# Attention and mixture of experts on one core: value products in two parts, maxima and statistics one at a time

## The chip, the cores and the metric

The kernel runs on one NeuronCore of a Trainium2 chip. The core has a matrix engine (TensorE, PE in the profile; its weight loads are shown as PEld), a vector engine (VectorE, DVE), a scalar engine (ScalarE, ACT), GpSimd (POOL) and an engine that mostly issues DMAs (SyncE, SP). [...] The metric is the device time of one execution in microseconds; the median of three runs is given.

## The reference

The input x has 2 sequences of 1024 positions and 256 channels, in float32. One layer is computed: causal attention with 16 query heads of 16 channels, 4 key and value heads and a linear position bias; a residual and a layer norm; then a mixture of 8 experts with the best one per token beside a shared expert; a residual and a second layer norm. Cut to what matters:

```python
q, k, v = x @ Wq, x @ Wk, x @ Wv              # 16 heads, 4 kv heads, 16 channels each
att = einsum("bhqd,bhkd->bhqk", q, k) / sqrt(16) + alibi + causal
att = softmax(att, axis=-1)
x = layernorm(x + einsum("bhqk,bhkd->bhqd", att, v) @ Wo)
logits = x @ router_w.T                       # the best expert, weighted by its sigmoid
routed = (up * silu(gate)) @ down             # of that expert
shared = (silu(x @ shared_gate) * (x @ shared_up)) @ shared_down
out = layernorm(x + shared + routed)
```

## The kernel before

The attention works on query tiles of 128 positions, 8 for each of the two sequences: `(b, qt)`. The softmax needs the maximum of each row before anything is exponentiated, so the scores are computed twice. Once as `s_ps` (queries on partitions, `start_s` and `end_s`, L403 to L469), only for the row maxima. Once as `t_ps` (keys on partitions, `start_t` and `end_t`, L497 to L539), with the maximum already subtracted by way of one more channel of the query (`qS`, L491), for the exponentials. One key tile of one query tile, `(b, qt, kt)`, is a step; there are 72 steps, the diagonal one first in each query tile.

The order of all instructions is written out by hand in Python. A counter `slot` goes up by one in every gap. For each step with scores still to be made there are two bursts, one per pair of kv heads, and after each a gap (L891 to L904). A burst is two `t_ps` matmuls for this step and two `s_ps` units for a query tile some steps ahead, interleaved. All four write PSUM banks of one pool of six (`ps_st`, tag `st`), taken in turn. ACT empties the `t_ps` banks: it exponentiates them into `pT` (L521), or, on the diagonal, copies them to `pD` (L524), which POOL masks (L526) before ACT exponentiates it (L538). DVE empties the `s_ps` banks with maximum reductions into `past` (L436). Where a unit holds a diagonal block, DVE (L449) and ACT (L451) also copy that block to `diag`; once it is complete, POOL masks one half of it, and DVE takes its four maxima (L466), one for each kv head, in slots that L464 and L465 fix by number.

`gap` (L813) puts other work between two bursts, in this order: what is due by its slot (`after_burst`, L770); at most one product that is due (`product`, L541); `join_maxima` and `spread_maxima` (L473, L483), which bring the row maxima into the query of a coming tile by way of the transposes `mT`; and one of the pieces of `finish` (L563), if there is room. A product multiplies the exponentials of one step with the values. It is four matmuls, one for each kv head, each 32 output partitions by 512 columns, into the accumulator `yT`, which is one PSUM bank of its own. When a query tile's last product is done, `finish` goes through its pieces in later gaps: a copy of `yT` to `y_raw`, four transposes `yq`, the division by the row sums (`y_n`), the transposes `ytp`, the output projection `o_ps`, the residual and the layer norm (`layernorm`, L223), the transposes `x1tp`, and the router's `lg`. With `room` at 0, no piece with PE work is placed; the old `gap` sets that after `mT`, and after a product when there is little to finish.

Ten bursts of `s_ps` alone come first, among the projections. When no scores are left to make, ten wide gaps (L825) hold the rest of the steps, each with one piece of the shared expert (`shared_pieces`, L695: `gu_sh`, `h_sh`, `dp_sh`), and last gaps (L842) the remainder. After `route` (L631) and the scatters of rows, the expert part (from L926) runs over the experts one by one, with the weights coming in by DMA.

## Time and profile before

| | |
|---|---|
| time, median of 3 runs | 580.52 us (579.5 to 581.03) |
| the profiled execution | 580.1 us, of which the span from the first to the last instruction is 578.3 us |
| mean granted TensorE clock | 0.99 |
| busy over the span | PE 552.6 us (96%), DVE 346.8 us (60%), ACT 266.8 us (46%), POOL 161.0 us (28%) |
| 0 to 56 us | projections and the ten leading bursts: PE 52.7 us busy, DVE 32.8, ACT 18.2 |
| 56 to 326 us | bursts and gaps |
| 326 to 428 us | wide gaps and the end of the attention: PE 101.0 us busy, DVE 45.7, ACT 42.8 |
| 428 to 578.3 us | experts: PE 131.8 us busy, DVE 59.9, POOL 73.1 |
| chain that ended last | PE 86%, DVE 6%, ACT 3% of the span |

The costliest groups of instructions are the two kinds of scores and what empties them. In this view a row has the line, engine, operation, what is written and read, the shape, the count, then the time in which at least one of them ran, the mean length of one in ns, and the idle time of the engine before them with what ended most of it.

```profile
L417 PE MATMUL s_ps<-kT,qT 32*128 32x512 f32 (+2 forms) x896 | 184.5, 470 | 1.8 <-ACT diag L451 0.8
L436 DVE TENSOR_REDUCE past<-s_ps 128x1 f32<-128x512 f32 (+3 forms) x256 | 148.0, 617 | 57.5 <-PE s_ps L417 50.1
L502 PE MATMUL t_ps<-qS,kT 32*128 32x512 f32 x576 | 168.4, 637 | 0.3 <-ACT pD L524 0.3
L521 ACT ACTIVATE pT<-t_ps 128x512 f32<-128x512 f32 x224 | 121.4, 600 | 76.3 <-PE s_ps L417 50.1
```

A float32 matmul of the program stands in the trace as two records: the 288 `t_ps` matmuls of the program are the 576 of L502. Matmuls that use different rows or columns of the array run at the same time, so the lengths of their records add up to more than the time they take; what counts is the distance from the start of one group to the start of the next.

### The profile page before, as it was taken

What the parts mean: (1) busy time and instruction counts of PE and PEld (TensorE: products, weight loads), DVE (VectorE), ACT (ScalarE), POOL (GpSimd) and SP (SyncE); (2) the same over time, 40 slices, a digit from 0 to 9 for tenths busy, and PEclk for the clock granted to TensorE, in tenths of its full rate; (3) what the DMA queues carried; (4) which work ended last, traced back from release to release, by engine and by line L of the source; (5) the groups of instructions that cost most, each with busy time, mean ns of one, the idle gap of its engine ahead of it and who ended that gap; (6) DMA issues with size and microseconds to landing.
All of it is one profiled execution on the core that took longest, in us unless ns stands there. A gap on an engine that the chain in (4) does not pass through costs nothing.

```text
span 578.3 us, 8805 instructions
## 1 busy us (share of the span) xinstructions
PE 552.6 (96%) x3292; PEld 305.5 (53%) x3292; DVE 346.8 (60%) x829; ACT 266.8 (46%) x509; POOL 161.0 (28%) x192
## 2 busy tenths in 40 slices
PE   8999999999999999999999999999999899999990
PEld 4655443534334353435345535446566788888650
DVE  2398968687696867688768733334542354544540
ACT  3432877657666756656667656461111111111120
POOL 5310511210201110114312301411020357776541
PEclk9999999999999999999999999999999999999996
DMA  6222850000000000000100000101071845552100
GB/s 201 42 34 36 233 180 2 2 1 0 2 1 1 1 1 1 2 2 31 44 1 1 1 1 19 56 0 38 8 278 57 285 150 173 183 194 71 46 17 3
DMA packets 24638, 34.72 MB, mean 60 GB/s; under 512 B 3806, under 2 KB 19460, under 8 KB 24592
## 3 DMA queue, kind: packets, MB, share of 16 engines
q1 hardware_dynamic: 20320, 27.38, 15.7%
q0 software_dynamic: 3456, 6.34, 3.1%
q8 instruction: 28, 0.46, 0.3%
q10 hardware_dynamic: 816, 0.39, 0.2%
q14 instruction: 18, 0.15, 0.1%
HBM read 22.20 MB, written 12.97 MB: 61 GB/s over the span
## 4 chain that ended last, share of the span: by engine, by line
PE 86%; DVE 6%; ACT 3%; issue 1%; DMA 1%; POOL 0%; POOLq 0%; ACTq 0%; DVEq 0%
PE t_ps L502 19%; PE yT L546 11%; PE s_ps L417 10%; PE gu_sh L705 6%; PE gp L1137 5%; PE dp L1153 5%; PE up L1137 5%; PE dp_sh L725 4%; PE o_ps L591 3%; DVE past L436 3%; PE qpj L291 3%; PE kpj L291 1%; PE mT L487 1%; PE dp L1195 1%; PE gp L1045 1%; PE lg L616 1%
## 5 line engine op out<-in xcount | busy, mean ns | idle before, releaser
L417 PE MATMUL s_ps<-kT,qT 32*128 32x512 f32 (+2 forms) x896 | 184.5, 470 | 1.8 <-ACT diag L451 0.8
L436 DVE TENSOR_REDUCE past<-s_ps 128x1 f32<-128x512 f32 (+3 forms) x256 | 148.0, 617 | 57.5 <-PE s_ps L417 50.1
L502 PE MATMUL t_ps<-qS,kT 32*128 32x512 f32 x576 | 168.4, 637 | 0.3 <-ACT pD L524 0.3
L521 ACT ACTIVATE pT<-t_ps 128x512 f32<-128x512 f32 x224 | 121.4, 600 | 76.3 <-PE s_ps L417 50.1
L417 PEld LDWEIGHTS s_ps<-kT,qT 32*128 32x128 f32 x896 | 79.3, 184 | 16.8 <-DVE past L436 4.9
L502 PEld LDWEIGHTS t_ps<-qS,kT 32*128 32x128 f32 x576 | 52.0, 183 | 59.4 <-issue 31.0
L231 POOL TENSOR_TENSOR rstd<-rstd,neg_half 128x1 f32<-128x1 f32 x36 | 20.5, 570 | 151.2 <-DVE rstd L230 149.7
L546 PE MATMUL yT<-pT,v 128*32 128x512 f32 x448 | 59.7, 605 | 0.0
L526 POOL TENSOR_SCALAR_AFFINE_SELECT pD<-pD 128x1024 f32<-128x1024 f32 x32 | 34.8, 1096 | 77.6 <-ACT pD L524 77.5
L524 ACT COPY pD<-t_ps 128x512 f32<-128x512 f32 x64 | 34.4, 600 | 20.0 <-PE s_ps L417 14.6
L705 PE MATMUL gu_sh<-x1T,sh_gu 128*128 128x512 f32 x96 | 43.6, 597 | 0.0
L237 POOL DMA_INDIRECT slot_x<-xs,slots x32 | 32.1, 1002 | 41.2 <-DVE slots L686 28.1
L454 POOL TENSOR_SCALAR_AFFINE_SELECT diag<-diag 128x1024 f32<-128x1024 f32 x16 | 17.5, 1097 | 92.9 <-ACT diag L451 92.9
L466 DVE TENSOR_REDUCE past<-diag 128x4 f32<-128x512 f32 x64 | 41.9, 676 | 0.0
L1145 ACT ACTIVATE sg<-gp 128x512 f32<-128x512 f32 x16 | 9.6, 597 | 54.6 <-PE gp L1137 44.3
L538 ACT ACTIVATE pD<-pD 128x1024 f32<-128x1024 f32 x32 | 34.3, 1072 | 0.4 <-POOL pD L526 0.4
L451 ACT COPY diag<-s_ps 128x128 f32<-128x128 f32 (+2 forms) x64 | 23.9, 377 | 22.5 <-DVE past L436 19.9
L1137 PE MATMUL gp<-slot_xT,wgu 128*128 128x256 f32 x128 | 30.4, 381 | 1.2 <-ACT slot_xT L1106 1.2
L449 DVE TENSOR_TENSOR diag<-s_ps,causal 128x128 f32<-128x128 f32 (+2 forms) x64 | 26.4, 415 | 7.1 <-PE s_ps L417 7.0
L1137 PE MATMUL up<-slot_xT,wgu 128*128 128x256 f32 x128 | 30.2, 379 | 0.0
L1153 PE MATMUL dp<-wd,slot_h 128*128 128x256 f32 x128 | 29.0, 379 | 0.0
L1082 POOL DMA_INDIRECT zt<-z_dram,row x20 | 20.6, 1032 | 27.8 <-issue 27.5
(171 smaller groups left out, 657.4 us busy)
## 6 DMA issues: line engine op xcount, KB each, us to landing
wgu<-_L_ffn_gate_up_proj_dram SPq DMA_DIRECT2D x8, 1024.0 KB
wd<-in_L_ffn_down_proj_dram SPq DMA_DIRECT2D x8, 512.0 KB
slot_x<-empty SPq DMA_DIRECT2D x1, 3900.0 KB
row<-slot_x SPq DMA_DIRECT2D x8, 260.0 KB
xs<-in_L_attn_x_dram SPq DMA_DIRECT2D x4, 512.0 KB
qT<-q_all SPq DMA_DIRECT2D x32, 64.0 KB
z_dram<-z_sh SPq DMA_DIRECT2D x12, 128.0 KB
row<-slot_x SPq DMA_DIRECT2D x4, 130.0 KB
```

The costliest lines, as they stand in the source:

```text
L417: lambda r=r: nc.tensor.matmul(sp[:, r * n * P : (r + 1) * n * P], lhsT=qT[b][rows, r0 + r, ts(qt, P)], rhs=kT[b][rows, key * P : (key + n ...
L436: nc.vector.tensor_reduce(past[:, h * HALF + j, heads, parts[b, qt][key]], sp[j][:, :, : past_n * P], AX.X, ALU.max, negate=True,)
L466: lambda g=g: nc.vector.tensor_reduce(past[:, g, :, 0], diag[:, g], AX.X, ALU.max, negate=True),
L502: lambda: nc.tensor.matmul(tp, lhsT=kT[b][rows, ts(kt, P)], rhs=qS[b, qt][rows].rearrange("p r q -> p (r q)"), start=True, stop=True,)
L521: nc.scalar.activation(p[:, j], tp[j], AF.Exp)
L524: nc.scalar.copy(p[:, j], tp[j])
L526: nc.gpsimd.affine_select(out=p, in_=p, pattern=[[0, HALF * REP], [1, P]], compare_op=ALU.is_ge, fill=MASKED, base=0, channel_multiplier=-1,)
L538: lambda: nc.scalar.activation(p, p, AF.Exp),
L546: nc.tensor.matmul(yTs[b, qt][g * PAD : (g + 1) * PAD], lhsT=vs[b][:, kt, g, :], rhs=p[:, g, :], start=start, stop=stop,)
L705: nc.tensor.matmul(gu[k], lhsT=sh_gu[:, c, col : col + P], rhs=x1T[:, c, ts(tb, TB)], start=(c == 0), stop=(c == KC - 1),)
L1137: nc.tensor.matmul(dst[:, j], lhsT=wgu[:, e, c, col : col + P], rhs=xT[:, c, :], start=(c == 0), stop=(c == KC - 1),)
L1153: nc.tensor.matmul(dp, lhsT=h[:, f, ts(i, P)], rhs=wd[:, e, f, :], start=(f == 0), stop=(f == FC - 1),)
```

## The change

A product becomes two, each over 256 of the 512 columns (`k` is 0 or 1), queued one slot apart. `gap` places one that is due, then maxima or a piece, and, if no piece with PE work was placed, a second one that has been due for a slot. The first half of a new query tile waits until two slots after the end of the tile before (`y_free`), since `yT` is one bank. In a wide gap up to two are placed together. A piece may now also stand in a gap with a product; the old rule that sets `room` to 0 after a product is gone.

The maxima of diagonal blocks (L466 before) go into a list, `chores`. At the end of each gap `chore` runs one of them, unless the slot is in `with_chore`: the slots in which DVE has a `qS` addition, a `y_n`, the residual after `o_ps`, or the statistics of a layer norm. What is left of them for a query tile runs at once when its maxima are joined, when a later tile needs the buffer of an older one, or before the first `gu_sh` piece. The statistics of the layer norm (`bn`, `mv`, `rstd`) move from the gap of `o_ps` to the next slot, and the normalization to two slots after that.

```diff
@@ -403,6 +403,9 @@
         def start_s(unit, h, j):
             b, qt, r0, nr, key, n = unit
             if (b, qt) not in rowmax:
+                for c in [c for c in chores if c[1] != next(reversed(rowmax))]:
+                    chores.remove(c)
+                    c[2]()
                 rowmax[b, qt] = (
                     mp.tile([P, N_KV, REP, P], F32, tag="diag", name="diag"),
                     mp.tile([P, N_KV, REP, 4], F32, tag="past", name="past", bufs=6),
@@ -461,17 +464,23 @@
                 channel_multiplier=1,
             )
             for g in range(N_KV):
-                at(
-                    slot + (1 + g // 2 if slot < 0 or (b and qt < 2) else 2 + g),
-                    lambda g=g: nc.vector.tensor_reduce(
-                        past[:, g, :, 0], diag[:, g], AX.X, ALU.max, negate=True
-                    ),
+                chores.append(
+                    (
+                        slot + (1 if slot < 0 else 2),
+                        (b, qt),
+                        lambda g=g: nc.vector.tensor_reduce(
+                            past[:, g, :, 0], diag[:, g], AX.X, ALU.max, negate=True
+                        ),
+                    )
                 )
 
         qS = {}
 
         def join_maxima(b, qt):
 
+            for c in [c for c in chores if c[1] == (b, qt)]:
+                chores.remove(c)
+                c[2]()
             past = rowmax.pop((b, qt))[1]
             nc.vector.tensor_reduce(
                 mnegs[qt % 2][:, :, :, ROW_MAX].rearrange("p r g -> p g r"),
@@ -490,6 +499,7 @@
             q = mp.tile([P, REP, P], F32, tag="qS", name="qS")
             nc.vector.tensor_add(q, qT[b][:, :, ts(qt, P)], mT)
             qS[b, qt] = q
+            with_chore.add(slot)
 
 
         probs, yTs = {}, {}
@@ -538,19 +548,23 @@
                 lambda: nc.scalar.activation(p, p, AF.Exp),
             )
 
-        def product(b, qt, kt, start, stop):
-            p = probs.pop((b, qt, kt))
-            if start:
+        def product(b, qt, kt, k, start, stop):
+            nonlocal y_free
+
+            p = probs[b, qt, kt] if k == 0 else probs.pop((b, qt, kt))
+            if start and k == 0:
                 yTs[b, qt] = ps_y.tile([P, 512], F32, tag="y", name="yT")
             for g in range(N_KV):
                 nc.tensor.matmul(
-                    yTs[b, qt][g * PAD : (g + 1) * PAD],
+                    yTs[b, qt][g * PAD : (g + 1) * PAD, ts(k, 256)],
                     lhsT=vs[b][:, kt, g, :],
-                    rhs=p[:, g, :],
-                    start=start,
-                    stop=stop,
-                )
-            if stop:
+                    rhs=p[:, g, ts(k, 256)],
+
+                    start=start and k == 0,
+                    stop=stop and k == 1,
+                )
+            if stop and k == 1:
+                y_free = slot + 2
                 posts.append([slot + 1, finish(b, qt)])
                 posts[-1].append(next(posts[-1][1]))
 
@@ -571,6 +585,7 @@
             yq = small_tile([P, REP, N_KV, PAD], "yq")
             for r in range(REP):
                 nc.tensor.transpose(yq[:, r].rearrange("p g d -> p (g d)"), y_raw[:, r, :], ident)
+            with_chore.add(slot)
             rs = stat.tile([P, REP, N_KV], F32, tag="rs", name="rs")
             nc.vector.reciprocal(rs, yq[:, :, :, HD])
             nc.vector.tensor_mul(
@@ -592,20 +607,24 @@
                     o_ps, lhsT=y_nT[:, c, :], rhs=wo_sb[:, c, :], start=(c == 0), stop=(c == KC - 1)
                 )
             nc.vector.tensor_add(xs[:, tt, :C], xs[:, tt, :C], o_ps)
-            norm = [layernorm(xs[:, tt, :C])]
-
-            def end_norm():
+            with_chore.add(slot)
+            norm = [lambda: norm.append(layernorm(xs[:, tt, :C]))]
+
+            def go_on():
                 if norm:
                     norm.pop()()
 
             if s_queue:
-                at(slot + 2, end_norm)
+                with_chore.add(slot + 1)
+                at(slot + 1, go_on)
+                at(slot + 3, go_on)
                 yield 1, 4
             else:
-                end_norm()
+                go_on()
+                go_on()
 
                 yield 1, 1 + slot % 2
-            end_norm()
+            go_on()
             tp = small_tile([P, KC, P], "x1tp")
             for c in range(KC):
                 nc.tensor.transpose(tp[:, c, :], xs[:, tt, ts(c, P)], ident)
@@ -697,6 +716,9 @@
 
             def gate_and_up(f):
                 if not h:
+
+                    while chores:
+                        chores.pop(0)[2]()
                     h.append(mp.tile([P, FC, TB], F32, tag="diag", name="h_sh"))
                 gu = [bank("gu_sh") for k in range(2)]
                 for k in range(2):
@@ -750,6 +772,9 @@
         s_queue = [u for b, qt in order for u in s_units(b, qt)]
         slot = 0
         deferred, posts, products = [], [], []
+
+        chores, with_chore = [], set()
+        y_free = 0
         seen, routed = set(), 0
         bursts_left = True
         tail = [p for tb in (0, 1, 3) for p in shared_pieces(tb)]
@@ -781,15 +806,17 @@
 
         def pieces(room, many=False):
 
+            made = False
             while True:
                 for p in posts:
                     if p[0] <= slot and p[2][0] <= room:
-                        if p[2][0] and not many:
-                            room = 0
+                        if p[2][0]:
+                            made = True
+                            room = room if many else 0
                         advance(p)
                         break
                 else:
-                    return
+                    return made
 
         def maxima():
             n = 0
@@ -810,16 +837,27 @@
                     posts[-1].append(next(posts[-1][1]))
                     routed += 1
 
+        def next_product(late):
+
+            if products and products[0][0] + late <= slot:
+                first_of = products[0][1][3:5] == (0, True)
+                if not (first_of and slot < y_free and bursts_left):
+                    product(*products.pop(0)[1])
+
+        def chore():
+            if slot not in with_chore and chores and chores[0][0] <= slot:
+                chores.pop(0)[2]()
+
         def gap(room):
             nonlocal slot
             after_burst()
             start_route(True)
-            full = bool(products) and products[0][0] <= slot
-            if full:
-                product(*products.pop(0)[1])
-            if maxima() or (full and len(posts) < 2):
-                room = 0
-            pieces(room)
+            next_product(0)
+            if maxima():
+                pieces(0)
+            elif not pieces(room):
+                next_product(1)
+            chore()
             slot += 1
 
         def wide_gap():
@@ -827,16 +865,18 @@
             nonlocal slot
             after_burst()
             start_route(False)
-            if products and products[0][0] <= slot + 1:
-                product(*products.pop(0)[1])
+            next_product(-1)
+            next_product(-2)
             if not maxima():
                 pieces(4)
+            chore()
             slot += 1
             after_burst()
             if tail:
                 tail.pop(0)()
             if not maxima():
                 pieces(4)
+            chore()
             slot += 1
 
         def last_gap():
@@ -884,10 +924,10 @@
             last = n + 1 == len(steps) or steps[n + 1][:2] != (b, qt)
             made = []
             if kt != qt:
-                made.append((2 * n + 2, (b, qt, kt, kt == 0, False)))
+                made += [(2 * n + 2 + k, (b, qt, kt, k, kt == 0, False)) for k in range(2)]
             if last:
                 ready = max(2 * n + 2, 2 * first[b, qt] + (7 if qt >= 3 else 4))
-                made.append((ready, (b, qt, qt, qt == 0, True)))
+                made += [(ready + k, (b, qt, qt, k, qt == 0, True)) for k in range(2)]
             if s_queue:
                 unit = s_queue.pop(0)
                 for h in range(2):
```

## The prediction

> **What bounds the kernel now.** I read the page's span row first, then the busy times by stage, then the timelines of TensorE (PE) and VectorE (DVE) inside the stage that the change touches. The span is 578.3 us in an execution of 580.1 us, so 1.8 us lie around it; the median of the runs shown is 580.52 us, 0.4 above, and I forecast against 580.1. The stage in which bursts of t_ps and s_ps alternate with gaps runs from 56 to 326 us:
>
> ```profile
> core 0: us, PE busy (x) PEld busy (x) DVE busy (x) ACT busy (x) POOL busy (x), PEclk, DMA share, GB/s
> 56.00:326.00 270.00, 267.14 (x1932) 118.33 (x1930) 208.49 (x453) 181.63 (x354) 53.19 (x56) 1.00 0.10 28
> ```
>
> PE looks full (267 of 270 us), DVE 77% and ACT 67%. That PE figure misleads: a burst that waits for a PSUM bank still has other matmuls in flight and counts as busy. The PE timeline shows it. Columns: start, length, engine, line, what, count.
>
> ```profile
> 161.25 0.69 PE L502 MATMUL t_ps<-qS,kT 32*128 32x512 f32 x1
> ...
> 162.32 0.44 PE L584 MATMUL ytp<-ident,y_n 128*128 128x128 f32 x2
> 162.69 0.69 PE L502 MATMUL t_ps<-qS,kT 32*128 32x512 f32 x1
> 163.06 0.69 PE L502 MATMUL t_ps<-qS,kT 32*128 32x512 f32 x1
> ...
> 164.24 1.06 PE L546 MATMUL yT<-pT,v 128*32 128x512 f32 x8
> ```
>
> The first burst starts at 161.25 and is over at 162.32: 1.07 us. The next starts at 162.69 and is over only at 164.24: 1.55 us for the same eight records. What it waited for is on DVE:
>
> ```profile
> 162.45 1.29 DVE L436 TENSOR_REDUCE past<-s_ps 128x1 f32<-128x512 f32 x2 [0.32 <-PE s_ps L417]
> 163.65 0.68 DVE L466 TENSOR_REDUCE past<-diag 128x4 f32<-128x512 f32 x1
> ```
>
> DVE begins to read s_ps 1.20 us after the burst began (162.45 against 161.25). With six banks and four per burst, the second half of a burst needs the first two banks of the burst before. They are read about 1.9 us after that burst began, and the next burst cannot end before 3.0 us after it (164.24 - 161.25 = 2.99). A gap with a product of 1.00 us hides this: 1.07 + 1.00 + 1.07 is more than 3.0. A short gap does not.
>
> I tallied the stage that way, each burst from its first matmul to the first of what follows, taking off 1.073 us. There are 124 bursts and gaps. Bursts at full speed come to 133.1 us, gap work to 98.0 us, waiting to 39.1 us; sum 270.2. The waiting by kind of gap before it: after a gap with a product (55 bursts) 5.0 us, 40 of them with nothing; after a gap with only small work (41) 15.6 us; where an empty gap lets two bursts meet (12 pairs) 15.0 us; the first four 3.4 us. Single means: x1tp alone 0.63, ytp alone 0.55, mT alone 0.37, yq alone 0.33, o_ps 0.0. **So PE sets the end, and 39 us of it is waiting behind DVE and ACT in gaps without a product.** That is what the change can win.
>
> **The change part by part.** *Products in two parts.* Today 60 products lie in these gaps. In the changed program's instruction order the 124 gaps hold 119 half products: 99 gaps with one, 10 with two, 15 with none. Price of a half:
>
> ```profile
> L546 PE MATMUL yT<-pT,v 128*32 128x512 f32 x448 | 59.7, 605 | 0.0
> ...
> 471.39 1.73 PE gp L1137 x8
> ```
>
> A product takes 1.00 us start to start (202.49 to 203.49), the mean of the 60 is 0.996. Its four column groups run side by side, so it is two passes of 512 columns; eight passes of 256 columns take 1.73 us in the second row, 0.216 each, so 0.86 us is streaming and 0.14 is the change of shape of the array. A half alone is two passes of 256: 0.43 + 0.14 = 0.57 us; two in one gap stay at 1.00. Gap products: 99 x 0.573 + 10 x 1.00 = 66.7 us against 59.8, so **+7 us**. The other gap work (mT, yq, ytp, o_ps, x1tp, lg, rank) is the same 38.3. The doubled weight loads are not charged: all eight of a product start within 0.16 us. Bounds for a half: 0.43 (no shape change; excluded, since every product row shows it) to 0.72 (shape change twice); I take 0.57, as its row is so near.
>
> [...] Bursts use four row groups, products four column groups and the transposes the whole array, so 109 gaps with a product instead of 60 are 49 more changes. The row prices one at 0.14 us: 6.9 us, which is the +7 above. [...]
>
> *What the waiting becomes.* PE's own work is now 133.1 + 66.7 + 38.3 = 238.1 us. The changed gaps by kind: 45 hold one half alone, 54 a half and another piece (0.94 us or more together), 10 two halves, 12 only yq, mT or rank, 3 are the empty ones at the start. For a half alone, walk the bank rule: burst at S, half, next burst could start at S+1.64 and end at 2.71, but ends at 3.0: wait 0.29. Its own first two banks were filled on time, DVE has read the first by about 3.5, and the half ends at 3.57, so the burst after that waits for nothing: mean 0.15. With a diagonal maximum in every gap DVE needs three times 0.60 us (that is the spacing of its instructions in the rows above, 163.65 to 164.25) = 1.8 us against PE's 1.64: wait 0.16. In gaps whose s_ps holds the diagonal block, DVE reads the first bank a third time after both reductions (L449), which gives a period near 2.0 and 0.36. Of the 45, 13 are of this last kind, so the walk gives 0.21; the nearest rows (mT, yq alone) say 0.35, but after bursts that a product had relieved. I take 0.27, between the two: 12.2 us. The 12 with yq, mT or rank at 0.35: 4.2. The 54 and the 10 at 0.08 (what gaps with a product show, 5.0 / 55 = 0.09): 5.1. The first three: 3.4. **Waiting 24.9 us, stage 263.0 us, 7.1 less than 270.1.** Bounds for the half alone: 0.10 (ACT and DVE never late) to 0.63 (what x1tp alone shows).
>
> *Diagonal maxima one at a time.* It is the same 64 instructions of L466 (676 ns each); none goes away. From 26 to 47.5 us, in the bursts ahead of the stage, DVE is busy almost throughout and the first join of maxima waits for it. Before, 12 of them stand ahead of that join, after it 8: four of 0.60 us leave. PE has 3.5 us of waiting there, so I count **-1.2 us** (bounds 0 and -2.4). They come back in the stage, where the 0.16 above already charges them. Seven are left over and run in one go at the start of the shared experts' part (4.2 us of DVE). What is queued behind them is the two h_sh products that empty the gu_sh banks; these banks are next needed some 6 us later, so nothing. If that cover fails, up to 2 us once.
>
> *Statistics in slots of their own.* bn, mv and rstd (0.76 us of DVE) leave the gap of o_ps, and the subtraction follows two slots later. It delays x1tp and the logits, which nothing in this stage waits for; the routing of the first group may move by a few gaps, but its scatters begin at 269 us and rows are fetched from 433 us on. Cost nothing; without that cover, the few gaps of 2 us each.
>
> *The end of the stage.* At 326 us 12.5 products are left instead of 12; in the wide gaps both halves stand together at 1.00 us, so PE's sum is the same. At the very end the accumulator yT (one bank) is turned over once more before the last transposes: one copy and its latency, **+0.5 us** (bounds 0 to 2). DMA issues and POOL's and SP's queues keep their order around scatters and loads; the expert part (428 us on) is PE-bound and moves as a whole.
>
> Sum: -7.1 - 1.2 + 0.5 = -7.8 us, 580.1 - 7.8 = 572.3; I forecast **572 us**.
>
> **Rivals.** *Slower: DVE has no gap left to catch up.* Today every second or third gap is 2.07 us long and DVE drains its queue in it (waits of DVE for s_ps come to 50.1 us in total, a sign of such slack). With near-equal gaps of 1.64 us and a maximum in most, a lateness once made would be carried from gap to gap. Price: if the 57 gaps with a half, yq, mT or rank alone wait 0.63 us as x1tp alone does, waiting is 35.9 + 5.1 + 3.4 = 44.4, the stage 282.5, the kernel 580.1 + 12.4 - 0.7 = 592 us. It decides from 0.41 us a gap on, where the stage is back at 270. For it: 0.35 is measured nearby. Against it: DVE's load per gap is 208.5 / 124 = 1.68 us, overlaps counted once, below the 1.92 us that PE needs on average (238.1 / 124).
>
> *No change:* waiting of 0.40 in those gaps, so the shape changes eat what the evenness gives: 580 us. For it, the +7 us is certain and the saving is not.
>
> *More than forecast:* 0.10 us in those gaps: 238.1 + 5.7 + 5.1 + 3.4 = 252.3, so 580.1 - 17.8 - 0.7 = 562 us. For it the walk's lower value; against it exponentials of 1.07 us on ACT (L538), two for each query tile, which also hold up t_ps banks.
>
> *The change does not even out:* the order shows 109 of 124 gaps with a half, so this is no case.
>
> **How the numbers follow.** A measurement of this kernel tells about 0.3% (1.7 us) from no change. Chances: my forecast (565 to 578 us) 0.50; more (below 565) 0.16; no change 0.10; slower 0.24. Faster is the first two, 0.66. The likeliest one's own range is 565 to 578. The range of 8 in 10 leaves out a tenth at each end: below, the half alone at 0.10 gives 562; above, half of the way into the slower rival, with 0.48 us a gap, gives 584.
>
> **What would show it.** Right: in the stage, yT rows of about 0.57 us start to start in nearly every gap; bursts after a lone half mostly between 1.07 and 1.4 us; no pairs of bursts meeting except at the start; the first t_ps a microsecond earlier; from 428 us on everything shifted alike. Wrong: a half at 0.7 or more (shape change under-priced), bursts of 1.5 to 1.7 after lone halves with DVE busy above 85% (the slower rival), or ACT's L538 in front of late t_ps reads.

## The result and the profile after

The changed kernel takes 585.93 us (median of 4 runs, 585.59 to 588.41), the kernel before, measured beside it on the same chip, 580.26 us. The ratio is 1.0107, with a 95% interval from 1.0076 to 1.0138: about 6 us slower, where 8 us faster had been forecast. The profiled execution took 585.59 us, with a span of 583.9 us. Line numbers are now those of the changed program: L512 is the old L502 (`t_ps`), L536 the old L526 (the masks of `pD`), L548 the old L538 (their exponentials), L558 the old L546 (products), L583 `y_raw`, L587 `yq`.

The page of the changed kernel, its span, PE's busy time and two groups of part 5:

```profile
span 583.9 us, 9953 instructions
...
PE 551.9 (95%) x3868; PEld 313.5 (54%) x3868; DVE 348.7 (60%) x829; ACT 266.4 (46%) x509; POOL 160.6 (28%) x192
...
L439 DVE TENSOR_REDUCE past<-s_ps 128x1 f32<-128x512 f32 (+3 forms) x256 | 147.6, 618 | 50.0 <-PE s_ps L420 37.9
...
L558 PE MATMUL yT<-pT,v 128*32 128x256 f32 x896 | 69.5, 390 | 0.0
```

The busy times by stage, in the window of the bursts and gaps:

```profile
56.00:326.00 270.00, 264.69 (x2402) 122.37 (x2402) 211.48 (x454) 181.38 (x354) 53.71 (x57) 1.00 0.10 28
```

DVE has 211.5 us in these 270 us, hardly more than before (208.5), and over the whole span it still waits 37.9 us for `s_ps` (50.1 before). It has not become the bound. PE is a little less busy than before (264.7 against 267.1 us), although the products cost more. To see where the time went I cut PE's timeline in both traces at the same instructions: the first `t_ps`, the first burst of a wide gap (bursts of `t_ps` alone, near 326 us), the last burst, the first `gp` matmul of the shared expert, and the first matmul of the routed experts.

| us | before | after | difference |
|---|---|---|---|
| start to the first `t_ps` | 56.06 | 55.88 | -0.2 |
| bursts and gaps | 270.09 | 271.05 | +1.0 |
| wide gaps, to the last burst | 57.81 | 62.38 | **+4.6** |
| last burst to the first `gp` | 45.05 | 45.71 | +0.7 |
| shared expert | 23.03 | 23.03 | 0 |
| routed experts, to the end | 126.27 | 125.83 | -0.4 |

Most of the loss lies in the wide gaps, a part of which the prediction had said only that its sum was the same. And the stage of bursts and gaps, where 7 us were to be won, has lost one. The wide gaps first. POOL and ACT in the timeline of the kernel before (start, length, engine, line, what; in brackets the idle time before it and what ended it):

```profile
368.45 1.04 POOL L237 DMA_INDIRECT slot_x<-xs,slots  x1 [12.18 <-DVE slots L686]
...
371.88 2.05 ACT L524 COPY pD<-t_ps 128x512 f32<-128x512 f32 x4 [2.61 <-PE t_ps L502]
372.37 0.98 POOL L237 DMA_INDIRECT slot_x<-xs,slots  x1 [0.30 <-issue]
373.35 2.16 POOL L526 TENSOR_SCALAR_AFFINE_SELECT pD<-pD 128x1024 f32<-128x1024 f32 x2
374.50 2.10 ACT L538 ACTIVATE pD<-pD 128x1024 f32<-128x1024 f32 x2
```

The same place in the changed kernel, all engines:

```profile
369.82 0.30 PE L681 MATMUL rank<-hot,before 128*128 128x32 f32 x2
...
371.44 2.05 ACT L534 COPY pD<-t_ps 128x512 f32<-128x512 f32 x4 [2.53 <-PE t_ps L512]
...
372.20 1.04 POOL L237 DMA_INDIRECT slot_x<-xs,slots  x1 [16.23 <-DVE mneg L485]
...
372.85 3.60 PE L727 MATMUL gu_sh<-x1T,sh_gu 128*128 128x512 f32 x8
...
376.08 0.97 POOL L237 DMA_INDIRECT slot_x<-xs,slots  x1 [0.30 <-issue]
376.28 0.60 PE L496 MATMUL mT<-ident,mneg 128*128 128x128 f32 x4
...
377.06 2.15 POOL L536 TENSOR_SCALAR_AFFINE_SELECT pD<-pD 128x1024 f32<-128x1024 f32 x2
...
378.20 2.10 ACT L548 ACTIVATE pD<-pD 128x1024 f32<-128x1024 f32 x2 [4.71 <-POOL pD L536]
380.20 0.58 ACT L735 ACTIVATE th<-gu_sh 128x512 f32<-128x512 f32 x1
...
380.81 0.69 DVE L736 SCALAR_TENSOR_TENSOR h_sh<-th,gu_sh 128x512 f32<-128x512 f32 x1 [7.05 <-ACT th L735]
...
382.21 0.68 DVE L500 TENSOR_TENSOR qS<-qT,mT 128x512 f32<-128x512 f32 x1
...
382.95 0.64 PE L599 MATMUL ytp<-ident,y_n 128*128 128x128 f32 x2 [3.99 <-DVE qS L500]
```

Read it from the bottom. PE stands 3.99 us ahead of `ytp`, for `qS` on DVE: `ytp` is written to the one PSUM bank of its pool (`ps_m`), which holds `mT` until `qS` has read it. `qS`, whose `mT` PE had made by 376.88, is late only because it stands behind `h_sh`, which waited 7.05 us for a `th` on ACT, and that `th`, whose `gu_sh` was over at 376.45, stands behind the exponentials of `pD`, which waited 4.71 us for their masks on POOL. The copies that the masks need were done at 373.5; POOL was then issuing the four scatters of the second group of rows, 1.3 us apart, until 377.05. So one lateness is handed on through four queues. In three of them work whose input was complete stands behind earlier work of its engine: the masks on POOL for 3.6 us (373.49 to 377.06), `th` on ACT for 3.75 (376.45 to 380.20), `qS` on DVE for 5.3 (376.88 to 382.21). A standstill of PE of 4.0 us hangs on it.

In both kernels the scatters stand directly ahead of the masks. But before, they were through when the copies came. The order was kept and its timing was not: in the changed kernel `lg` of that group's last tile comes one wide gap later (359.68 against 353.89 us), and `rank` falls into the second half of its wide gap, behind 3.5 us of `gu_sh` (369.82 against 366.21), so the slots and with them the scatters come 3.7 us later.

And PE pays twice. The busy times by stage again, from 383.0 to 386.5 us; the number before the last two is the granted PE clock:

```profile
383.00:386.50 3.50, 3.50 (x6) 1.73 (x7) 0.00 (x0) 0.37 (x1) 0.00 (x0) 0.51 0.00 0
```

Right after the standstill PE's clock is at half for 3.4 us. The `gu_sh` that follows takes 4.97 us from start to start instead of 3.44. So the standstill costs 4.0 us and the half clock 1.5 more.

Now the stage of bursts and gaps. A lone half and a pair of halves in PE's timeline:

```profile
214.80 0.64 PE L558 MATMUL yT<-pT,v 128*32 128x256 f32 x8
215.37 0.69 PE L512 MATMUL t_ps<-qS,kT 32*128 32x512 f32 x1
...
216.44 0.64 PE L558 MATMUL yT<-pT,v 128*32 128x256 f32 x8
216.90 0.61 PE L558 MATMUL yT<-pD,v 128*32 128x256 f32 x8
217.44 0.69 PE L512 MATMUL t_ps<-qS,kT 32*128 32x512 f32 x1
```

215.37 - 214.80 = 0.57 us for a half alone, 217.44 - 216.44 = 1.00 for two: the forecast prices, to the hundredth. Gap products come to 68.4 us (forecast 66.7), other gap work to 38.6 (38.3), bursts to 133.1. The waiting is 31.0 us where 24.9 was forecast. The largest part of that excess is in one kind of place, here on ACT and PE:

```profile
218.60 1.08 ACT L531 ACTIVATE pT<-t_ps 128x512 f32<-128x512 f32 x2 [0.93 <-PE s_ps L420]
219.57 1.06 ACT L548 ACTIVATE pD<-pD 128x1024 f32<-128x1024 f32 x1
220.51 0.59 ACT L583 COPY y_raw<-yT 128x512 f32<-128x512 f32 x1
...
221.16 0.66 PE L587 MATMUL yq<-ident,y_raw 128*128 128x128 f32 x4 [0.65 <-ACT y_raw L583]
```

The last half product of the tile starts at 218.51 and its records end at 219.15, so `yT` is complete before 219.57. But a diagonal exponential of the next tile stands ahead of the copy `y_raw` on ACT, and `yq` waits for the copy. The burst before this `yq` (from 219.08) takes 2.08 us instead of 1.07. Of the nine such bursts in the stage five wait 1.0 us, one 1.2 and one 0.6; the nine come to 7.2 us. In the kernel before, the bursts ahead of the nine `yq` that stand alone in a gap wait 0.15 us on the mean; `y_raw` follows the copies of `pD` there, and no exponential stands in front of it:

```profile
217.36 1.07 ACT L524 COPY pD<-t_ps 128x512 f32<-128x512 f32 x2 [1.65 <-PE s_ps L417]
218.41 0.59 ACT L569 COPY y_raw<-yT 128x512 f32<-128x512 f32 x1
219.49 1.08 ACT L521 ACTIVATE pT<-t_ps 128x512 f32<-128x512 f32 x2 [0.49 <-PE t_ps L502]
```

### The profile page after: what moved, and what is told of

It reads as the page before. It is cut to its first block, busy times and chain, and to the rows that moved or that the text cites. A ratio compares the mean times of both kernels' runs of the same rounds, so it can differ in the third digit from the quotient of the medians.

```text
span 583.9 us, 9953 instructions
## 1 busy us (share of the span) xinstructions
PE 551.9 (95%) x3868; PEld 313.5 (54%) x3868; DVE 348.7 (60%) x829; ACT 266.4 (46%) x509; POOL 160.6 (28%) x192
## 4 chain that ended last, share of the span: by engine, by line
PE 87%; ACT 4%; DVE 3%; issue 2%; POOL 1%; DMA 1%; POOLq 0%; DVEq 0%; ACTq 0%
PE t_ps L512 20%; PE yT L558 12%; PE s_ps L420 8%; PE gu_sh L727 7%; PE gp L1177 5%; PE dp L1193 5%; PE up L1177 5%; PE dp_sh L747 4%; PE o_ps L606 3%; PE qpj L291 2%; PE yq L587 2%; PE lg L635 1%; ACT pD L548 1%; PE kpj L291 1%; ACT pT L531 1%
## 5 line engine op out<-in xcount | busy, mean ns | idle before, releaser
L420 PE MATMUL s_ps<-kT,qT 32*128 32x512 f32 (+2 forms) x896 | 180.4, 470 | 1.2 <-ACT diag L454 0.8
L439 DVE TENSOR_REDUCE past<-s_ps 128x1 f32<-128x512 f32 (+3 forms) x256 | 147.6, 618 | 50.0 <-PE s_ps L420 37.9
L512 PE MATMUL t_ps<-qS,kT 32*128 32x512 f32 x576 | 160.6, 639 | 0.7 <-DVE diag L452 0.4
L558 PE MATMUL yT<-pT,v 128*32 128x256 f32 x896 | 69.5, 390 | 0.0
L512 PEld LDWEIGHTS t_ps<-qS,kT 32*128 32x128 f32 x576 | 47.3, 183 | 40.3 <-issue 23.1
L536 POOL TENSOR_SCALAR_AFFINE_SELECT pD<-pD 128x1024 f32<-128x1024 f32 x32 | 34.8, 1093 | 86.0 <-ACT pD L534 86.0
L558 PEld LDWEIGHTS yT<-pT,v 128*32 128x32 f32 x896 | 18.7, 108 | 65.1 <-issue 60.7
L727 PE MATMUL gu_sh<-x1T,sh_gu 128*128 128x512 f32 x96 | 45.3, 616 | 0.0
L548 ACT ACTIVATE pD<-pD 128x1024 f32<-128x1024 f32 x32 | 34.1, 1070 | 4.9 <-POOL pD L536 4.9
```

Of the source, the lines that this page charges most:

```text
L420: lambda r=r: nc.tensor.matmul(sp[:, r * n * P : (r + 1) * n * P], lhsT=qT[b][rows, r0 + r, ts(qt, P)], rhs=kT[b][rows, key * P : (key + n ...
L439: nc.vector.tensor_reduce(past[:, h * HALF + j, heads, parts[b, qt][key]], sp[j][:, :, : past_n * P], AX.X, ALU.max, negate=True,)
L512: lambda: nc.tensor.matmul(tp, lhsT=kT[b][rows, ts(kt, P)], rhs=qS[b, qt][rows].rearrange("p r q -> p (r q)"), start=True, stop=True,)
L536: nc.gpsimd.affine_select(out=p, in_=p, pattern=[[0, HALF * REP], [1, P]], compare_op=ALU.is_ge, fill=MASKED, base=0, channel_multiplier=-1,)
L548: lambda: nc.scalar.activation(p, p, AF.Exp),
L558: nc.tensor.matmul(yTs[b, qt][g * PAD : (g + 1) * PAD, ts(k, 256)], lhsT=vs[b][:, kt, g, :], rhs=p[:, g, ts(k, 256)],  start=start and k == 0,
```

## The experiments

Two causes were to be told apart from the rivals of the prediction: the scatters ahead of the masks (POOL) and the exponential ahead of `y_raw` (ACT), against DVE without slack, against statistics that delay the routing, and against halves that simply gain nothing. Each kernel has its own median and its ratio to the kernel before, measured beside it, with the 95% interval; stage and tail are the second and third rows of the table above. The last column says whether PE's clock is at half for 3.4 us somewhere between 380 and 388 us.

| kernel | median us | ratio to before | stage us | tail us | half clock in the tail |
|---|---|---|---|---|---|
| before | 580.26 | 1 | 270.09 | 57.81 | no |
| changed | 585.93 | 1.0107 [1.0076, 1.0138] | 271.05 | 62.38 | yes |
| a_scatter | 578.07 | 0.9971 [0.9958, 0.9984] | 269.44 | 56.62 | no |
| b_yraw | 582.9 | 1.0044 [1.0029, 1.006] | 269.78 | 62.40 | yes |
| c_both | 576.6 | 0.9946 [0.9932, 0.9959] | 267.94 | 56.62 | no |
| e_oldmax | 586.27 | 1.0117 [1.0099, 1.0135] | 271.71 | 62.41 | yes |
| f_halves | 586.05 | 1.0101 [1.0077, 1.0124] | 270.34 | 62.23 | yes |
| g_whole | 578.61 | 0.9972 [0.996, 0.9984] | 269.05 | 58.21 | no |
| k_bscat | 580.48 | 1.0001 [0.9987, 1.0014] | 270.09 | 57.67 | no |
| d_exp | 574.66 | 0.9894 [0.987, 0.9918] | 265.42 | 56.62 | no |
| i_all | 573.55 | 0.9876 [0.985, 0.9902] | 265.42 | 56.62 | no |
| l_wexp | 580.94 | 1.0009 [0.9996, 1.0022] | 271.72 | 58.21 | no |
| m_expo | 583.2 | 1.004 [1.0021, 1.006] | 268.64 | 62.40 | yes |
| n_after | 586.74 | 1.0111 [1.0086, 1.0136] | 272.29 | 62.41 | yes |

**The scatters behind the masks.** One more turn in `route` for the second group; POOL's order changes in this one place, no other engine's at all.

```diff
             nc.vector.tensor_copy(slots[:, ts_], slot_f)
+            if k == 1:
+                yield 0, 1
             for tt in range(t0, t0 + n):
```

> The changed kernel with one thing moved: the four scatters of the second routing group stand on POOL behind the two masks of pD of that stretch, not ahead of them. PE, ACT, DVE and SP keep their order. If the queue of POOL makes the end of the attention late (theory), the wait of 4.0 us on PE near 382 us and the slower gu_sh after it go, and the time falls from 585.9 by 4 to 5.5 us, to about 581; the stage from 56 to 327 us stays at 271. If the loss comes from shape changes or from DVE having no gap to catch up (rivals), it moves by less than 1.5 us.

Measured: 578.07 us, 7.9 less than the changed kernel and below the kernel before. Its timeline at the same place (lines behind 706 have moved by two):

```profile
369.80 2.05 ACT L534 COPY pD<-t_ps 128x512 f32<-128x512 f32 x4 [2.54 <-PE t_ps L512]
...
370.94 2.14 POOL L536 TENSOR_SCALAR_AFFINE_SELECT pD<-pD 128x1024 f32<-128x1024 f32 x2 [16.62 <-ACT pD L534]
...
372.07 2.10 ACT L548 ACTIVATE pD<-pD 128x1024 f32<-128x1024 f32 x2 [0.22 <-POOL pD L536]
...
373.26 1.04 POOL L237 DMA_INDIRECT slot_x<-xs,slots  x1 [0.18 <-issue]
...
377.24 0.44 PE L599 MATMUL ytp<-ident,y_n 128*128 128x128 f32 x2
```

The masks start 1.1 us after the first copy and not 5.6 us after it, the exponentials wait 0.22 us instead of 4.71, and `ytp` waits for nothing. The tail is 5.8 us shorter, which is the standstill of 4.0, the half clock of 1.5 and 0.2 us in small pieces. The later scatters cost nothing. So the wide gaps' loss is shown to be this order on POOL. The expectation was some 2 us short of the gain of 7.9. Of this shortfall, 1.6 us are in the stage: at 273.6 us the changed kernel has a halt that a_scatter has not. Its cause is open (last section), so of the 7.9 us only the 5.8 of the tail are shown to be POOL's order.

**`y_raw` ahead of the exponential.** In `gap`, a last half that is due goes ahead of `after_burst`; ACT's order changes in seven places.

```diff
         def gap(room):
             nonlocal slot
+            ends = bool(products) and products[0][0] <= slot
+            ends = ends and products[0][1][3] == 1 and products[0][1][5]
+            if ends:
+                next_product(0)
             after_burst()
             start_route(True)
-            next_product(0)
+            if not ends:
+                next_product(0)
```

> The changed kernel with one thing moved: where the last half product of a query tile and the exponential of a pD fall into the same gap, ACT copies yT to y_raw ahead of that exponential (7 places); PE, DVE, POOL and SP keep their order. Theory: yq waits for y_raw behind an exponential of 1.06 us, about 1.0 us in each of 8 gaps, so the stage of bursts and gaps falls from 271 to about 265 us and the time from 585.9 to about 580; the wait near 382 us stays. Rivals (DVE late, shape changes): under 1.5 us.

> The changed kernel with both moves (scatters behind the masks, y_raw ahead of the exponential). Theory: the two add up, 585.9 - 5 - 6 = 575 us, which is faster than the kernel before by about 5 us and near the forecast of 572. If something else than these two queues costs the time, it stays above 582.

Measured: 582.9 us alone, and 576.6 us together with the scatters, where 580 and 575 were expected. The two traces without a half clock or halt in the stage, a_scatter and c_both, give its worth: 1.5 us of stage. The waiting ahead of the nine `yq` falls from 7.2 to 3.4 us, as expected, but in the bursts behind them it rises from 1.4 to 4.8: the exponential, now behind `y_raw`, delays the reads of their `t_ps`. Most of the wait was only moved.

**The maxima back in their old slots**, the rest as changed; only DVE's order differs. `chores.append(...)` becomes the `at(...)` of before.

> The changed kernel with the maxima of diagonal blocks in their old slots (the halves of products and the statistics stay as changed); only DVE's order differs. Rival (DVE has no gap left to catch up because a maximum stands in most gaps): at least 5 us faster than the changed kernel. Theory: the maxima are not what costs, so within 2 us of 585.9 either way; my prediction counted -1.2 us for moving them, so perhaps 1 us slower.

Measured: 586.27 us against 585.93. The near tie hides something: the changed kernel's trace has the halt of 1.6 us, this one has none. Against a_scatter, which has the same stage as the changed kernel but for the halt, e_oldmax has a stage 2.3 us longer (271.71 against 269.44). So beside halves the maxima one at a time gain about 2 us in the stage, and bunching them as before helps nothing: DVE, with a maximum in most gaps, is not what the halves suffer from. The slower rival of the prediction falls.

**Halves alone, and the other two parts alone.** f_halves has the halves with the old maxima and the old norm; PE, ACT and POOL have the order of the changed kernel. g_whole has the maxima and the statistics with whole products in the old `gap`; PE and ACT have the order of the kernel before.

> This kernel has the halves alone: products in two parts of 256 columns, but the diagonal maxima in the slots of before and the norm statistics with their o_ps as before. PE, ACT and POOL have the order of the changed kernel, only DVE's differs. Theory (the halves alone shift rank behind gu_sh and so the scatters ahead of the masks; maxima and statistics are worth nothing that can be measured): 586 us, within 1.5 of the changed kernel, with the second group's four scatters again ahead of the masks of pD and about 62.4 us from the first wide burst to the last. Rival (the statistics' slots delay the logits and with them the routing): the scatters come at 368 to 372 us as before, the masks wait for nothing, 581 us. Rival (DVE is relieved by maxima one at a time): 588 us or more here.

> This kernel has whole products of 512 columns in the gaps of before, with the diagonal maxima one at a time and the norm statistics in slots of their own. PE and ACT have the order of the kernel before. Theory (these two parts of the change are worth nothing that can be measured): 580 us, within 1.5 of before, tail from the first wide burst to the last within 1 us of 57.8. Rival (they carry the loss): 584 to 586 us. Rival (they carry a gain which the halves give back): 576 to 578 us.

Measured: 586.05 and 578.61 us. The halves carry the whole loss, `rank` behind `gu_sh` and the late masks with them: the summary of waits of f_halves has the same 4.7 us as the longest wait of its exponentials for their masks.

```profile
ACT pD L545 <- POOL pD L533: 4.9, 2, 4.7
```

So the statistics' slots, which by name delay the routing, are not what moved it. The other two parts are a gain of 1.6 us and not nothing, 0.5 us in the lead and 1.0 in the stage of that trace; the expectation of g_whole, within 1.5 us of before, stands at its edge.

**The same order on POOL in the kernel before.** A turn of two slots in `route`, so that the scatters stand behind the masks there too.

> This kernel is the one before with the second group's four scatters behind the two masks of pD on POOL; nothing else moves on any engine. In the kernel before the first mask starts at 373.35 us, directly behind the fourth scatter, though its pD copy was done at about 371.9: about 1.0 us late. Theory (the masks stand behind the scatters in both kernels, and each us of it goes to the end): 579.3 us, 0.5 to 1.2 us less than before, and the tail from the first wide burst to the last falls from 57.8 to about 56.7. Then halves and their company are worth 1 to 1.5 us once both kernels have the same POOL order. Rival (a mask that is 1 us late is covered by PE's work in the wide gaps): no difference, 580.3 us, and the halves are worth 2 us. Rival (the later scatters delay the rows fetched for the experts): slower, 581 us or more; against it the fetches begin at 433 us, 55 us later.

Measured: no difference. I had read the first mask's start, directly behind a scatter, as a late start; with the scatters out of the way it starts 0.3 us earlier, counted in each trace from the first wide burst (46.9 us after it against 47.2). The order that costs the changed kernel 5.8 us cost the kernel before nothing, because the scatters came 3.7 us earlier there. The queue's order had no price by itself here (ratio 1.0001).

**The exponentials further apart.** On top of a_scatter, the first of the two diagonal exponentials of a tile goes one slot earlier. Each counts from its own part's slot, so they are now three slots apart instead of two (the expectation counts one less).

```diff
             at(
-                slot + (3 + h if qt >= 3 else 1),
+                slot + (2 + 2 * h if qt >= 3 else 1),
                 lambda: nc.scalar.activation(p, p, AF.Exp),
             )
```

> This kernel is the changed one with the second group's scatters behind the two masks of pD (as in a_scatter, 578.07 us) and, besides, the first of the two diagonal exponentials of a query tile (the h = 0 part of pD, 1.06 us on ACT) one slot earlier, so that two exponentials of one query tile stand two slots apart instead of one. Only ACT's order differs from a_scatter. Theory (ACT's long exponentials in front of y_raw and of late t_ps reads cost about 0.4 us more than forecast in eight gaps): the stage of bursts and gaps falls from 269.4 to about 267.5 us and the time to 576 us. Rival (ACT only moves its work; the wait comes back at another burst, as b_yraw showed inside the stage): 578 us, stage 269 to 270. Slower rival (the earlier exponential now waits for its mask on POOL and holds up ACT's queue): 579 to 581 us.

Measured: 574.66 us, stage 265.42, 4.0 us less than in a_scatter. ACT at the tile shown above, now:

```profile
217.35 1.06 ACT L548 ACTIVATE pD<-pD 128x1024 f32<-128x1024 f32 x1
218.39 1.08 ACT L531 ACTIVATE pT<-t_ps 128x512 f32<-128x512 f32 x2
219.36 0.59 ACT L583 COPY y_raw<-yT 128x512 f32<-128x512 f32 x1
220.03 1.08 ACT L531 ACTIVATE pT<-t_ps 128x512 f32<-128x512 f32 x2
```

The exponential has gone into an earlier gap in which ACT had 0.9 us free, `y_raw` follows the burst's reads at once, and nothing is behind it. The waiting ahead of the nine `yq` falls from 7.2 to 3.5 us, 3.7 of the stage's 4.0, and none of it comes back behind them.

> d_exp with, besides, y_raw placed on ACT ahead of the exponentials of the burst behind a query tile's last half product (the edit of b_yraw); only ACT's order differs from d_exp. In d_exp the bursts ahead of yq wait 0.28 to 0.64 us, 0.46 on the mean of nine. Theory (what is left there is half y_raw behind one pair of exponentials, half the bank rule of 0.28 that every lone half has): two to three gaps of 0.3 us each are won and nothing more: 573.5 to 574.5 us, stage 264.5 to 265.4. Rival (the wait moves to the burst behind yq, as in b_yraw): 574.7 us, bursts behind yq waiting 0.5. Slower rival (y_raw ahead makes t_ps reads late everywhere): 576 us.

i_all turned out to be no new variant: in d_exp `y_raw` already stands ahead, and the edit of b_yraw finds nothing to move; all engines have the same order in both. It is a second measurement of d_exp, 573.55 us with the same stage to the hundredth, and shows how far two measurements of one order lie apart: about 1 us. These two are the fastest version found, 6 to 7 us below the kernel before.

> g_whole (whole products of 512 columns, maxima and statistics in slots of their own, 578.61 us) with the first of the two diagonal exponentials of a query tile one slot earlier, as in d_exp; only ACT's order differs from g_whole. In g_whole two bursts meet ahead of seven of the yq and wait 1.24 us there. Theory A (the waiting there is y_raw behind the exponential, as in the halves): 7 times 0.4 to 0.6 us go, 575 to 576 us, and the halves are worth little even then. Theory B (where two bursts meet, the four s_ps and t_ps banks and DVE's reads of them set the wait, and ACT's order costs nothing there): 578 to 579 us, and the gain of d_exp is to be had with halves alone. Slower rival: 580 us or more, if the earlier exponential holds up t_ps reads ahead of meeting bursts.

Measured: 580.94 us, 2.3 more than g_whole; the slower rival held. (The pairs of bursts that meet stand behind `yq`, and not ahead of it as the expectation says.) With whole products the earlier slot is one where two bursts meet, and the exponential stands there in front of `t_ps` reads that are already late: four of those pairs wait 0.3 to 0.7 us longer. So the slot that suits the halves hurts the whole products.

**Both causes apart from each other, and the changed kernel again.**

> The changed kernel with the first diagonal exponential of a query tile one slot earlier, as in d_exp, and with the second group's scatters left ahead of the masks of pD; only ACT's order differs from the changed kernel. Theory (the two causes are independent: POOL's order costs 5.7 us in the tail, ACT's order 3.5 to 4 us in the stage): 582 to 582.5 us, stage 3.5 to 4 us shorter than in the changed kernel, tail from the first wide burst to the last 62.4 us. Rival (most of what d_exp won was tied to POOL's order): 585 us. Rival (with ACT earlier the tail's wait shrinks too): 579 us, tail under 61.

> The changed kernel once more, unaltered, to see whether the halt at 273.6 to 275.2 us of its first profiled execution (PE, ACT and DVE stand for 1.6 us there, and no row names what released them) belongs to the kernel or to that execution. If to the kernel: 585.9 us again and the halt at the same instructions. If to single executions: runs spread over 584 to 588 us, and the profiled one has its halt elsewhere or none; the 7.9 us between the changed kernel and a_scatter are then 5.8 of POOL's order and up to 2 of chance.

Measured: 583.2 us with the earlier exponential alone, where 582 to 582.5 was expected; the tail is 62.40, as with the old exponentials. The stage is only 2.4 us shorter than in the changed kernel (268.64 against 271.05), because m_expo's trace has a half-clock stretch there besides the halt; against n_after, whose trace has both, it is 3.65 us shorter. So the two causes add up, within a microsecond. The unaltered changed kernel gives 586.74 us, and its halt is at the same instruction again.

## Why the prediction was wrong

**The step that failed** is the one that said of the routing that it "may move by a few gaps" at no cost, and of the queues that "POOL's and SP's queues keep their order around scatters and loads". For a move of the routing it asked only who waits for the scattered rows (nobody for 60 us). It did not ask what is queued behind the scatters on POOL. There stand the masks, behind these ACT's exponentials and `th`, behind these `h_sh` and `qS`, and then PE. a_scatter and f_halves show it: 5.8 us in the tail, which the sum had at nothing. The step also expected the move from the statistics and in the first group. What cost came from the halves, and in the second; the first group's `rank` came earlier instead (255.12 against 264.84 us).

**The second step is a term of the right kind and the wrong size**: 0.27 us of waiting at a half alone, 0.08 where two stand together. The 55 bursts after halves without other work wait 0.39 us on the mean, 21.4 us together where these two figures give 13; nearly all of it stands behind the 45 lone halves, 0.46 us each. Some 5 us of it are the bursts ahead of `yq`, where a last half comes one slot later than the whole product did and `y_raw` so falls behind a diagonal exponential. The walk of the bank rule looked at DVE and at PSUM banks, and left ACT out; the prediction named ACT's exponentials only against a larger gain and as a sign to look for, and charged them nothing. d_exp shows what was missing. With both orders mended, the stage's waiting is 25.8 us (forecast 24.9), the stage 265.4 (forecast 263.0), and the time 573.55 to 574.66 us where 572 was forecast. That the sums come so near is in part luck: the lone halves of d_exp still wait 0.39 us each (17.7 us where 12.2 were forecast), and all other bursts together wait less than forecast (8.1 against 12.7). What the lone halves still wait for was not taken apart. The account of PE's own work was sound; the queues beside it were not read.

Of the 13.6 us between the forecast's sum (572.3) and the result, 8.0 are in the stage (6.1 of waiting, 1.7 of products, the halt of 1.6 within them), 4.6 in the wide gaps and 1.0 in the lead.

**The other points.** Prices of a half and of a pair: right. The 0.14 us for a change of shape was an estimate from two rows of the trace before (1.00 us for a product, less 0.86 for its passes), and as a price it held: a half takes 0.57 us (0.43 and 0.14), and two together, which pay it once, 1.00. That it goes with the shape fits the changed kernel's trace, where `gu_sh`, with `mT` of the same shape 128*128 behind it, takes 3.43 us from start to start (372.85 to 376.28) for eight passes of 512 columns, 0.43 each and nothing over; no run took it apart. Products 68.4 us against 66.7, in part by the halt (67.9 in a_scatter). Maxima out of the lead: measured from the first `qpj` (at 7.21 us before, 7.47 after) to the first `t_ps`, to leave out what stands ahead of it, 48.85 us before and 48.41 after (48.86 in e_oldmax), so -0.4 where -1.2 was forecast; that the four instructions leave is right, but PE's wait there was mostly for something else. Statistics: f_halves against e_oldmax differs by them alone, 586.05 against 586.27 us, so nothing beyond the noise, as forecast, though in their traces the stage with the statistics apart is 1.4 us longer. Leftover maxima ahead of `gu_sh`: no wait in the trace, right. End of the stage: +0.7 against +0.5. The rival of no change priced 0.40 us of waiting in the 57 gaps with a lone half, `yq`, `mT` or `rank`; the trace shows 0.41 there, so the stage did what this rival said, and the loss beyond it is the wide gaps'. The slower rival was on the right side, but its mechanism, DVE without slack, fell with e_oldmax.

**What the halves are worth** depends on the order beside them. With only POOL's order mended they stand at 578.07 us, whole products with the same maxima and statistics at 578.61. With the exponentials spread it is 574.66 against 580.94. The best order of ACT for whole products was not searched, so 4 to 5 us (573.55 or 574.66 against 578.61) is what is shown between the best of each that was tried.

## What to carry to other kernels

When a change moves a step by a slot, follow it through every queue that it stands in (here POOL's, ACT's and DVE's, where work with its input complete stood 3.6 to 5.3 us behind earlier work), and ask for each what is behind it and when that becomes ready; "nobody needs its result yet" is only half of the question. An unchanged order is no safety: the scatters ahead of the masks cost 5.8 us in the changed kernel and nothing in the kernel before, where they came 3.7 us earlier. And when work is spread more evenly on one engine, the long instructions of its neighbours (here exponentials of 1.06 us, whose place was worth 4.0 us of the stage in d_exp) have to be laid out anew before the change is judged.

## What the runs showed of the hardware

**A standstill of PE costs more than itself.** All six kernels with the 4 us standstill in the tail have PE's clock at half for 3.4 us right behind it, and none of the other eight has. In the changed kernel the half clock lasts 3.41 us, and in the 3.41 us ahead of it PE's records are busy for 0.10 us. From 383.0 to 386.5 us a_scatter has the full clock, as it has in all of its trace from 5 to 564 us:

```profile
383.00:386.50 3.50, 3.50 (x26) 1.64 (x23) 0.68 (x3) 2.38 (x5) 1.80 (x3) 1.00 0.00 0
```

But not every half-clock stretch here has a standstill of PE ahead of it. n_after has a second one at 278.1 us, m_expo at 274.8 and b_yraw one of 6.8 us at 60.3 us, and in the 3.41 us ahead of these PE's records are busy for 3.04, 2.92 and 3.06 us. The first two begin 3 to 3.5 us after the halt described next, but the changed kernel has the same halt and keeps its full clock. What set them stays open.

**A halt that no row explains.** In the changed kernel, n_after and m_expo the copy `x1T` of one tile, whose transposes on PE start in the first of them at 273.15, comes there at 275.23 and is followed by reads of `t_ps` and `s_ps` that are as late:

```profile
272.67 1.08 ACT L531 ACTIVATE pT<-t_ps 128x512 f32<-128x512 f32 x2 [1.43 <-PE s_ps L420]
275.23 0.37 ACT L631 COPY x1T<-x1tp 128x256 f32<-128x256 f32 x1 [1.47 <-PE s_ps L420]
276.63 1.08 ACT L531 ACTIVATE pT<-t_ps 128x512 f32<-128x512 f32 x2 [1.03 <-PE lg L635]
```

In the other seven kernels with halves the copy follows 0.5 us after the start of the transposes and not 2.1, with the same instructions around it. The halt belongs to the program and not to a single execution, it is worth 1.6 us, and it is not the scatters' order alone, since b_yraw, e_oldmax and f_halves have that order and no such halt. A load of 16 KB of instructions begins at 274.7 us in the changed kernel's trace, but one also begins 0.7 to 1.9 us after this copy in the seven without the halt, so its presence does not tell them apart. What causes the halt stays open; no run was made for it beyond the repeat.
